# The forget gate's token products of a two-layer fused kernel: seven half-width blocks for each pair of sequences instead of plain products

## The chip, the cores and the metric

The kernel runs on one core of one Trainium2 chip. The metric is device time in microseconds (us) of one execution. The inputs are drawn once, with a fixed seed, and all arrays are float32.

## The reference, cut to what matters

The whole computation is two layers of a network on 32 sequences of 128 tokens with 512 channels. Most of it (a mixture of experts, a feed-forward part chosen per sequence, a second mixture of experts) comes before the part that the change touches and is left as it is. The last part is a recurrence that steps over the 32 sequences; each step treats all 128 tokens of one sequence as a batch:

```python
c0 = jnp.broadcast_to(in_c, (batch, in_c.shape[0]))
def step(c, xt):                       # xt: 128 tokens x 512
    ft = jax.nn.sigmoid(xt @ wf.T + c @ uf.T + bf)
    it = jax.nn.sigmoid(xt @ wi.T + c @ ui.T + bi)
    gt = jnp.tanh(xt @ wc.T + c @ uc.T + bc)
    c = ft * c + it * gt
    return (c, None)
c_final, _ = lax.scan(step, c0, x)
h = jnp.tanh(jnp.einsum('tbi,oi->tbo', x, wo) + c_final @ uo.T + bo)
```

The products `xt @ w.T` (called token products here) do not depend on the state `c`; the products `c @ u.T` do. So the token products can be made ahead of their step, or for two steps at once, and the others can't.

## The kernel before, in words

**Numbers.** Every float32 matrix operand is split into a rounded high part and a remainder (`split`: ACT copies the high part, L64; DVE subtracts, L65). A product is then three TensorE matmuls, high by high, high by low and low by high (`mm3`, L95), summed in PSUM. One matmul takes a stationary block of 128 x 128 (the tokens or the state) and a moving block of up to 512 weight columns. With 512 channels a full product is 4 blocks x 3 = 12 matmuls of 512 columns.

**Order.** The program is written as straight Python; a scheduler of the framework orders each engine's queue at compile time, by the order of the program and by when it reckons the operands and buffers ready. `tc.issue_after(x)` and `queue_behind(i, x)` put an instruction behind another on its engine's queue by hand; they are no waits on the chip beyond the order of the queue. `behind(both)` does this for the two instructions (ACT's and DVE's) of a split.

**The recurrence.** A step `t` has these parts:

- `from_c(t, n, ...)`: the state's product of gate n (c, i, f), 12 matmuls of 512 columns into a bank of PSUM (pool `ps_g`, 3 banks, tile `ps_c`, `ps_i`, `ps_f`).
- `gate(t, n, ...)`: DVE adds the bias or the token part out of PSUM (L1720), ACT applies the sigmoid or tanh (L1721), and for i DVE multiplies by the tanh gate (L1723).
- `new_c`: DVE multiplies f by the old state (L1726) and adds i times g (L1728). The last instruction is kept in `made`.
- `turn`: TensorE transposes the new state (4 transposes, tile `ptC`, L1647) and `split` makes the stationary operand `cT` of the next step.
- `gate_y(t + 3)` prepares the tokens of a later sequence: fetched rows times a gate (DVE, L1612), 4 transposes (tile `ptF`, L1620), a copy (L1626), a split into `zA`. `sums_z` makes, for every second sequence, the sums of token blocks that the seven-block form needs (DVE, L1637 to L1641), split into `zS`.

**Token products of c and i before.** Two steps 2n and 2n+1 and the gates c and i are taken together as a 2 x 2 product of blocks: rows are the two steps, the inner index is the two halves of 256 channels, columns are the gates c and i. That is done with seven block products (Winograd's form of Strassen's scheme) instead of eight. Each block product is 2 x 3 = 6 matmuls of 512 columns into a bank of the pool `ps_b` (3 banks, tiles `pA11`, `pA12`, `pS1` and so on, shown as `pA` and `pS`). `first_of_pair` makes five of them before the turn into an even step; its sums run on DVE at L1690 to L1695. `second_i` makes S3 T3 before the turn into an odd step, and its two sums (L1705, L1706) are put behind `made`; `second_c` makes A22 T4 after that turn (sum at L1711). The weights' combinations (T1 to T4) are formed once at the start, in `rest_of_weights`, during steps 0 and 1. Steps 0 and 1 use plain products.

**Token products of f before.** `plain(t + 1, ps, "f", True, False)` puts the 12 matmuls of f for the next step into the bank of `ps_f`, where `from_c` adds the state's product later. Only the bias is added by `gate`. It stands before the turn into an odd step and after the turn into an even step.

**The end.** After the last steps the tokens of all sequences are read back (`z_d`), four groups of 512 at a time, split (tile `zF`) and multiplied by `wo` (tile `poF`, function `unit`), and the last state by `uo` (tile `cu`). `wo` is fetched and split in step 28 into a buffer of the pool `zp`; the first group's tokens are fetched there too.

## Time and profile before

| what | value |
|---|---|
| time, 3 runs | median 2416.92 us, 2414.24 to 2421.07 |
| the profiled execution | 2416.54 us, its span 2414.9 us, so 1.6 us lie outside the span |
| granted TensorE clock, mean | 0.999 |
| TensorE matmul busy | 2393.2 us, 99% of the span |
| VectorE (DVE) busy | 1485.1 us, 61% |
| ScalarE (ACT) busy | 1079.8 us, 45% |
| recurrence in the trace | first state product at 1777.94 us, last at about 2315 us |

"Span" is the time from the first to the last instruction in the profile. TensorE (PE) has two rows: PE for the matmuls, PEld for loading the stationary block, which overlaps. A matmul's shown duration is its latency through a pipeline; what it costs a full engine is the distance from start to start. A group of lines in the timeline is a run of alike instructions on an engine, with its start, its length and the count after the x; a bracket at the end tells how long the engine was idle before it, and whom it waited for.

### The profile page before, as it was taken

Reading aid. Unit: us, or ns where it says so; the run is one execution under the profiler, and the core shown is the slowest. Engines: PE = TensorE matmul, PEld = TensorE weight load, DVE = VectorE, ACT = ScalarE, POOL = GpSimd, SP = SyncE. Lnnn points to the kernel's source line nnn. Section 1 sums busy time; section 2 is a strip of 40 time slices with the busy share of each in tenths; the row PEclk is TensorE's granted clock in tenths of the full one; section 3 lists DMA queues with packets and bytes.
Section 4 is the critical chain, followed back from the end, with each engine's and each line's share of the span. In section 5 each row is a group of like instructions: output and inputs, shape, how many; then the busy total and the mean of one; then the engine's idle time right before and its main releaser. Section 6 shows DMA issues by size and latency. Waiting matters only on the chain.

```text
span 2414.9 us, 36797 instructions
## 1 busy us (share of the span) xinstructions
PE 2393.2 (99%) x12792; PEld 2028.2 (84%) x12792; DVE 1485.1 (61%) x2548; ACT 1079.8 (45%) x1897; POOL 417.4 (17%) x461
## 2 busy tenths in 40 slices
PE   9999999999999999999999999999999999999999
PEld 6788888888887888888888889999988888888887
DVE  8797644456567445446455477776756666666664
ACT  5544633343223545445455466666643223223242
POOL 1000022222233233323222120000010000000012
PEclk9999999999999999999999999999999999999999
DMA  6445555457564334343243287677642111111165
GB/s 219 150 131 170 184 171 167 151 188 254 175 222 156 128 128 130 106 132 110 86 151 125 90 297 253 226 224 233 196 156 63 49 44 53 49 44 49 53 238 181
DMA packets 196383, 357.93 MB, mean 148 GB/s; under 512 B 37665, under 2 KB 70481, under 8 KB 193633
## 3 DMA queue, kind: packets, MB, share of 16 engines
q1 hardware_dynamic: 148224, 258.57, 32.0%
q0 software_dynamic: 36448, 75.95, 10.6%
q10 hardware_dynamic: 11520, 20.98, 2.4%
q8 instruction: 107, 1.75, 0.3%
q14 instruction: 84, 0.68, 0.1%
HBM read 377.08 MB, written 91.80 MB: 194 GB/s over the span
## 4 chain that ended last, share of the span: by engine, by line
PE 78%; DMA 1%; DVE 1%; issue 1%; ACT 1%; ACTq 0%; POOL 0%; DVEq 0%; POOLq 0%
PE phD L95 7%; PE poD L95 7%; PE po L95 7%; PE ps_f L95 7%; PE p L95 6%; PE pb L95 4%; PE ps_i L95 4%; PE ps_c L95 4%; PE poF L95 3%; PE pS L95 3%; PE pv L95 3%; PE acc L95 3%; PE pA L95 2%; PE pur L95 2%; PE por L95 2%
## 5 line engine op out<-in xcount | busy, mean ns | idle before, releaser
L65 DVE TENSOR_TENSOR wD<-rawD,wD 128x1024 fp32r<-128x1024 f32 x128 | 156.5, 1229 | 77.6 <-ACT wD L64 77.5
L95 PE MATMUL p<-xhl,swu 128*128 128x512 f32 x768 | 190.6, 400 | 5.7 <-ACT xhl L64 5.7
L95 PE MATMUL p<-xhl,kept_u 128*128 128x512 f32 x768 | 184.6, 394 | 1.2 <-DVE kept_u L65 0.7
L95 PEld LDWEIGHTS phD<-xe,wD 128*128 128x128 f32 x1536 | 183.2, 188 | 1.3
L95 PE MATMUL phD<-xe,wD 128*128 128x256 f32 x1536 | 183.5, 279 | 0.0
L95 PE MATMUL poD<-wD,hD 128*128 128x512 f32 x768 | 181.5, 392 | 0.0
L95 PEld LDWEIGHTS p<-xhl,swu 128*128 128x128 f32 x768 | 145.7, 192 | 36.8 <-ACT xhl L64 5.9
L95 PEld LDWEIGHTS p<-xhl,kept_u 128*128 128x128 f32 x768 | 141.9, 188 | 31.3 <-DVE kept_u L65 1.1
L95 PEld LDWEIGHTS poD<-wD,hD 128*128 128x128 f32 x768 | 141.9, 188 | 28.3
L64 ACT CAST wD<-rawD 128x1024 fp32r<-128x1024 f32 x128 | 133.6, 1047 | 52.7 <-PE poD L95 31.0
L305 POOL DMA_INDIRECT xg<-in_x_rows_dram,blk_t x71 | 68.1, 960 | 439.0 <-PE ptx L315 242.0
L1587 POOL DMA_INDIRECT y<-res_d,gat_i x32 | 35.8, 1118 | 472.9 <-DVE r L1612 394.3
L95 PE MATMUL pur<-r,xb 128*128 x792 | 110.6, 288 | 3.3 <-issue 1.5
L65 DVE TENSOR_TENSOR xb<-ptx,xb 128x512 fp32r<-128x512 f32 x68 | 47.0, 691 | 106.1 <-ACT xb L64 102.7
L95 PE MATMUL por<-r,hbr 128*128 x396 | 107.6, 407 | 0.5 <-ACT hbr L64 0.5
L95 PEld LDWEIGHTS pur<-r,xb 128*128 128x128 f32 x792 | 98.6, 188 | 5.6 <-issue 2.7
L95 PE MATMUL ps_c<-uc_hl,cT 128*128 128x512 f32 x384 | 96.3, 399 | 0.0
L95 PE MATMUL pb<-rT,Wo_hl 128*128 128x256 f32 x768 | 94.7, 281 | 0.3 <-DVE rT L65 0.2
L95 PE MATMUL ps_f<-wf_hl,z 128*128 128x512 f32 x384 | 94.5, 394 | 0.0
L95 PE MATMUL acc<-kept_d,as 128*128 128x512 f32 x384 | 93.6, 392 | 0.4 <-DVE as L65 0.2
L844 POOL DMA_INDIRECT o<-o_d,s_i x64 | 64.7, 1011 | 168.0 <-PE pth L864 82.9
L95 PE MATMUL pv<-w_recept_hl,xr 128*128 128x512 f32 x384 | 93.7, 392 | 0.0
(1048 smaller groups left out, 5130.5 us busy)
## 6 DMA issues: line engine op xcount, KB each, us to landing
rawD<-in_w_key_dram SPq DMA_DIRECT2D x64, 512.0 KB
rawD<-in_w_value_dram SPq DMA_DIRECT2D x64, 512.0 KB
swr<-in_sw_dram SPq DMA_DIRECT2D x120, 256.0 KB
o_d<-obr SPq DMA_DIRECT2D x66, 256.0 KB
rraw<-in_rw_dram SPq DMA_DIRECT2D x32, 256.0 KB
xc<-in_x_dram SPq DMA_DIRECT2D x32, 256.0 KB
hid_d<-o ACTq DMA_DIRECT2D x32, 256.0 KB
xh_d<-xc SPq DMA_DIRECT2D x32, 256.0 KB
```

The costliest lines, as they stand in the source:

```text
L64: first = nc.scalar.copy(hi, src).ins
L65: done = nc.vector.tensor_tensor(lo, src, hi.bitcast(F32), ALU.subtract).ins
L95: done = nc.tensor.matmul(ps, lhsT=left(hl, k), rhs=right(hr, k), start=start and k + n == 0, stop=stop and 3 * k + n == last,)
L305: nc.gpsimd.indirect_dma_start(out=xg[i], out_offset=None, in_=a["x_rows"], in_offset=bass.IndirectOffsetOnAxis(ap=blk_t[:, i : i + 1], ax ...
L844: nc.gpsimd.indirect_dma_start(out=o[n], out_offset=None, in_=o_d, in_offset=bass.IndirectOffsetOnAxis(ap=idx[:, b : b + 1], axis=0),)
L1587: got = nc.gpsimd.indirect_dma_start(out=y, out_offset=None, in_=res_d, in_offset=bass.IndirectOffsetOnAxis(ap=gat_i[:, b : b + 1], axis=0),)
```

## The change

The token products of f are made with seven blocks too, for two steps at once. Rows are again the two steps and the inner index the two halves of the channels; the columns are now the two halves of f's own 512 columns, so a block product is 6 matmuls of 256 columns. The two sequences of the first pair, and of the second, are made plainly (`plain_f`): with the weights kept as blocks, where the second half of the columns of the upper channels is held as the sum B11 + T1, that takes 30 matmuls of 256 columns for each sequence. The products no longer add up in the bank of `ps_f`; they go to banks of `ps_b`, and DVE adds them to a tile `fs[t]`, which `gate` then adds to `ps_f` in place of the bias.

Around that: `f_start` (A11 B11, A12 B21) and `f_second` (S3 T3) stand before the turn into an odd step, `f_third` (A22 T4) after it, `f_first` (S1 T1, S2 T2, S4 B22) after the turn into an even step; the sums of `f_start`, `f_second` and `plain_f` are queued behind the split of `cT`. f's weights are split in seven pieces of 512 elements per partition instead of two of 1024, three of them in `rest_of_weights`. `zA` loses the block A21 (kept for the first pair alone), `zS` has one buffer, which first holds f's raw weights, `sums_z` uses the tile `y` as its scratch, so `get_y` comes after it, and `hl` moves to another pool. At the end `wo`'s split moves from step 28 to step 30 and into the room that the token weights leave, two of the first group's four loads go with it, `uo`'s splits are put behind the first group's and behind the last state, and the last turn behind two of the first `unit`s.

```diff
+        BLOCKS = {(0, 0): 0, (0, 1): 1, (1, 1): 2}
+        def tokens(n, j, half):
+            return zA[n][:, BLOCKS[j, half]] if (j, half) in BLOCKS else a21[0]
...
+                zA[n] = zp.tile([P, 3, 2, K2, P], FR, tag="z", name=f"z_{n}")
...
-            s = gp.tile([P, 2, K2, P], F32, tag="sz", name=f"sz_{n}")
+            zS[n] = zp.tile([P, 4, 2, K2, P], FR, tag="zs", bufs=1, name=f"zs_{n}")
+            s = spare[2 * n + 1].rearrange("p (s k q) -> p s k q", s=2, k=K2)
...
+        def blocks_f(n, *todo):
+            ps = ps_b.tile([P, 2, HD], F32, tag="b", name=f"pf{todo[0][0]}_{n}")
+            for i, (which, w) in enumerate(todo):
+                left = left_of(which, n)
+                mm3(ps[:, i], lambda h, k: left[:, h, k, :], lambda h, k: wf[w][:, h, k, :], K2)
+            return ps
...
+        def f_start(n):
+            f1, p1 = f_tile(2 * n)
+            ps = blocks_f(n, ("A11", "B11"), ("A12", "B21"))
+            return [
+                nc.vector.tensor_tensor(p1, ps[:, 0], bias["f"][:, :HD], ALU.add).ins,
+                nc.vector.tensor_tensor(f1, ps[:, 1], p1, ALU.add).ins,
+            ]
+        def f_first(n, room):
+            u, v = room[:, :HD], room[:, HD:]
+            p1 = fs[2 * n][:, HD:]
+            ps = blocks_f(n, ("S1", "T1"), ("S2", "T2"))
+            last = blocks_f(n, ("S4", "B22"))
+            with tc.issue_after(made[0]):
+                nc.vector.tensor_tensor(v, ps[:, 0], bias["f"][:, HD:], ALU.add)
+                nc.vector.tensor_tensor(u, ps[:, 1], p1, ALU.add)
+                nc.vector.tensor_tensor(v, v, u, ALU.add)
+                nc.vector.tensor_tensor(p1, last[:, 0], v, ALU.add)
+            f_done[n] = u, v
...
-            v[n] = gp.tile([P, D], F32, tag="v" + n, name=f"v_{n}_{t}")
+            v[n] = fs.pop(t) if n == "f" else gp.tile([P, D], F32, tag="v" + n, name=f"v_{n}_{t}")
...
+            nc.vector.tensor_tensor(f22, f22, f12, ALU.subtract)
+            split_f("T2", f22)
+            nc.vector.tensor_tensor(f11, f22, f11, ALU.subtract)
+            nc.vector.tensor_tensor(f21, f21, f22, ALU.subtract)
+            split_f("T3", f11)
+            split_f("T4", f21)
...
-                plain(1, ps, "f", True, False)
+                plain_f(1)
             elif t < NB - 1:
                 if odd:
                     second_i(n)
-                    plain(t + 1, ps, "f", True, False)
+                    rest, adds = f_second(n) if n > 1 else (None, [])
+                    if n + 1 < NB // 2:
+                        adds += f_start(n + 1)
                 else:
                     first_of_pair(n)
+                    adds = [plain_f(t + 1)] if n == 1 else []
                 cT_next = turn(c, t + 1)
+                for i in adds:
+                    queue_behind(i, last_split[1])
                 if odd:
                     second_c(n)
+                    if rest:
+                        f_third(n, *rest)
+                elif n == 1:
+                    plain_f(t + 2)
...
                 else:
-                    plain(t + 1, ps, "f", True, False)
+                    f_first(n, rooms.pop(n))
...
+            if t == NB - 2:
+                sx.close()
+                sz.close()
+                op = sf.enter_context(tc.tile_pool(name="op", bufs=1, side="right", **kw))
...
+                for k, raw in enumerate(raws):
                     split(wo1[:, 0, k], wo1[:, 1, k], raw)
...
+        ahead = [unit(0, o) for o in range(KD)]
+        for i in turned_c:
+            queue_behind(i, ahead[1])
```

More of the change, by code (lines that the diff above doesn't have):

```diff
@@ L156, in tile_kernel @@
     used_i = const.tile([P, 1], I32, name="used_i")
-    hl = const.tile([P, KD, NB], F32, name="hl")
     bo3 = const.tile([P, KD], F32, name="bo3")
@@ L830, in tile_kernel @@
         new_i = po_p.tile([P, NB], I32, name="new_i")
+        hl = po_p.tile([P, KD, NB], F32, name="hl")
         ones = po_p.tile([P, P], F32, name="ones2")
@@ L1601, in tile_kernel @@
             first_got = get_y(b)
-        zp = sf.enter_context(tc.tile_pool(name="zp", bufs=2, **kw))
-        zA, zS, zts = {}, {}, {}
+        sz = sf.enter_context(ExitStack())
+        zp = sz.enter_context(tc.tile_pool(name="zp", bufs=2, **kw))
+        zA, zS, zts, a21 = {}, {}, {}, []
+        BLOCKS = {(0, 0): 0, (0, 1): 1, (1, 1): 2}
+        def tokens(n, j, half):
+            return zA[n][:, BLOCKS[j, half]] if (j, half) in BLOCKS else a21[0]
+        spare = {}
         def gate_y(b):
@@ L1613, in gate_y @@
             if j == 0:
-                z = zp.tile([P, 2 * KD * D], FR, tag="z", name=f"z_{n}")
-                zA[n] = z[:, : KD * D].rearrange("p (j h k q) -> p j h k q", j=2, h=2, k=KD)
-                zS[n] = z[:, KD * D :].rearrange("p (s h k q) -> p s h k q", s=4, h=2, k=K2)
+                zA[n] = zp.tile([P, 3, 2, K2, P], FR, tag="z", name=f"z_{n}")
                 zts[n] = first_p.tile([P, 2, KD, P], F32, tag="cT0", name=f"zt_{n}")
@@ L1623, in gate_y, with split_tokens @@
             zt = zts[n][:, j]
+            def split_tokens(t):
+                if j == 0:
+                    t = t.rearrange("p (a k) q -> p a k q", a=2)
+                    split(zA[n][:, 0:2, 0], zA[n][:, 0:2, 1], t)
+                    return
+                if n == 0:
+                    a21.append(gp.tile([P, 2, K2, P], FR, tag="a21", name="a21"))
+                    split(a21[0][:, 0], a21[0][:, 1], t[:, :K2])
+                split(zA[n][:, 2, 0], zA[n][:, 2, 1], t[:, K2:])
             if b < LEAD:
-                split(zA[n][:, j, 0], zA[n][:, j, 1], pt)
+                split_tokens(pt)
             nc.scalar.copy(zt, pt)
@@ L1629, in gate_y @@
             if b >= LEAD:
-                split(zA[n][:, j, 0], zA[n][:, j, 1], zt)
+                split_tokens(zt)
+            spare[b] = y
         def sums_z(n):
@@ L1645, in turn @@
             pt = ps_c.tile([P, KD, P], F32, tag="t", name=f"ptC_{t}")
-            for k in range(KD):
-                nc.tensor.transpose(pt[:, k, :], c[:, bass.ts(k, P)], ident)
+            turned_c[:] = [
+                nc.tensor.transpose(pt[:, k, :], c[:, bass.ts(k, P)], ident).ins for k in range(KD)
+            ]
             cT = gp.tile([P, 2, KD, P], FR, tag="cT", name=f"cT_{t}")
@@ L1653, in bank, with left_of @@
             return ps_g.tile([P, D], F32, tag="g", name=f"ps_{n}_{t}")
+        def left_of(which, n):
+            if which[0] == "S":
+                return zS[n][:, int(which[1]) - 1]
+            return tokens(n, int(which[1]) - 1, int(which[2]) - 1)
         def block(which, w, n):
-            s = {"A11": (0, 0), "A12": (0, 1), "A22": (1, 1)}.get(which)
-            if s is None:
-                left = zS[n][:, int(which[1]) - 1]
-            else:
-                left = zA[n][:, s[0], :, s[1] * K2 : (s[1] + 1) * K2]
+            left = left_of(which, n)
             ps = ps_b.tile([P, D], F32, tag="b", name=f"p{which}_{n}")
@@ L1664, in block, with f_tile @@
             return ps
+        HD = D // 2
+        def blocks_f(n, *todo):
+            ps = ps_b.tile([P, 2, HD], F32, tag="b", name=f"pf{todo[0][0]}_{n}")
+            for i, (which, w) in enumerate(todo):
+                left = left_of(which, n)
+                mm3(ps[:, i], lambda h, k: left[:, h, k, :], lambda h, k: wf[w][:, h, k, :], K2)
+            return ps
+        fs, f_done = {}, {}
+        def f_tile(t):
+            pool, tag = (gp, "vf") if t % 2 or t == 0 else (first_p, "c0")
+            fs[t] = pool.tile([P, D], F32, tag=tag, name=f"v_f_{t}")
+            return fs[t][:, :HD], fs[t][:, HD:]
@@ new lines, in plain_f @@
+        def plain_f(t):
+            n, j = divmod(t, 2)
+            f_tile(t)
+            ps = ps_b.tile([P, 2, HD], F32, tag="b", name=f"pf_{t}")
+            for i, todo in enumerate((((0, "B11"), (1, "B21")), ((0, "B11"), (0, "T1"), (1, "B22")))):
+                for m, (half, w) in enumerate(todo):
+                    z = tokens(n, j, half)
+                    mm3(
+                        ps[:, i], lambda h, k: z[:, h, k, :], lambda h, k: wf[w][:, h, k, :], K2,
+                        m == 0, m == len(todo) - 1,
+                    )
+            return nc.vector.tensor_tensor(fs[t], ps.rearrange("p i n -> p (i n)"), bias["f"], ALU.add).ins
@@ new lines, in f_start @@
+        def f_start(n):
[4 more added lines that the diff above has]
+                nc.vector.tensor_tensor(f1, ps[:, 1], p1, ALU.add).ins,
+            ]
+        def f_first(n, room):
[9 more added lines that the diff above has]
+            f_done[n] = u, v
@@ L1666, in plain, with f_second, f_third @@
+        def f_second(n):
+            f1, f2 = f_tile(2 * n + 1)
+            u, v = f_done.pop(n)
+            ps = blocks_f(n, ("S3", "T3"))
+            adds = [
+                nc.vector.tensor_tensor(u, ps[:, 0], u, ALU.add).ins,
+                nc.vector.tensor_tensor(f2, ps[:, 0], v, ALU.add).ins,
+            ]
+            return (f1, u), adds
+        def f_third(n, f1, u):
+            nc.vector.tensor_tensor(f1, blocks_f(n, ("A22", "T4"))[:, 0], u, ALU.add)
         def plain(t, ps, which, start, stop):
@@ L1671, in plain @@
                 "i": ((0, "B11"), (0, "T1"), (1, "B22")),
-                "f": ((0, "f0"), (1, "f1")),
             }[which]
@@ L1676, in plain @@
             for m, (half, w) in enumerate(todo):
-                z = zA[n][:, j, :, half * K2 : (half + 1) * K2]
+                z = tokens(n, j, half)
                 done = mm3(
@@ L1682, in plain @@
             return done
-        half_done, made = {}, []
+        half_done, made, rooms, turned_c = {}, [], {}, []
         def first_of_pair(n):
@@ L1689, in first_of_pair @@
             p1, u, v = first[:, 0], first[:, 1], second[:, 0]
+            rooms[n] = second[:, 1]
             nc.vector.tensor_tensor(p1, block("A11", "B11", n), bias["c"], ALU.add)
@@ L1729, in new_c @@
             return new
+        names = ("T4", "T3", "T2", "B22", "T1", "B21", "B11")
+        f_all = shifted(wx_p, len(names) * K2 * D, tag="wf", name="wf_hl")
+        f_all = f_all.rearrange("p (w h k n) -> p w h k n", w=len(names), h=2, k=K2)
+        wf = {n: f_all[:, i] for i, n in enumerate(names)}
         wt = {
             n: wx_p.tile([P, 2, K2 * D], FR, tag="w" + n, name=f"w{n}_hl")
-            for n in ("T4", "T3", "T2", "f1", "B22", "T1", "B21", "B11", "f0")
+            for n in names
         }
@@ L1761, in tile_kernel, with split_f @@
         for n in "cif":
-            from_c(0, n, ps, cT, True, False)
-        f01 = zp.tile([P, 2 * KD * D], F32, tag="z", name="raw_wf")
-        f01 = [f01[:, bass.ts(h, K2 * D)] for h in range(2)]
+            from_c(0, n, ps, cT, True, n == "f")
+        raw_f = zp.tile([P, KD, D], F32, tag="zs", bufs=1, name="raw_wf")
         with tc.issue_after(first_got):
             for h in range(2):
-                nc.gpsimd.dma_start(out=f01[h], in_=a["wf"].rearrange("p k n -> p (k n)")[:, bass.ts(h, K2 * D)])
+                s = slice(h * K2, (h + 1) * K2)
+                nc.gpsimd.dma_start(out=raw_f[:, s], in_=a["wf"][:, s])
+        f11, f12, f21, f22 = (raw_f[:, h * K2 : (h + 1) * K2, bass.ts(i, HD)] for h in range(2) for i in range(2))
+        def split_f(n, raw):
+            split(wf[n][:, 0], wf[n][:, 1], raw)
         gate_y(0)
@@ L1773, in tile_kernel @@
         with behind(first_z):
-            for h in range(2):
-                split_part(f"f{h}", f01[h])
+            split_f("B11", f11)
+            split_f("B21", f21)
+            nc.vector.tensor_tensor(f12, f12, f11, ALU.subtract)
+            split_f("T1", f12)
+            split_f("B22", f22)
         for b in range(LEAD):
@@ L1798, in tile_kernel @@
                 with tc.issue_after(done):
-                    plain(0, ps, "f", False, True)
+                    plain_f(0)
+                more["f"] = fs[0]
                 for n in "cif":
@@ L1802, in tile_kernel @@
             else:
+                more["f"] = fs[t]
                 for n in "cif":
@@ L1821, in tile_kernel @@
                     second_i(n)
-                    plain(t + 1, ps, "f", True, False)
+                    rest, adds = f_second(n) if n > 1 else (None, [])
+                    if n + 1 < NB // 2:
+                        adds += f_start(n + 1)
                 else:
                     first_of_pair(n)
+                    adds = [plain_f(t + 1)] if n == 1 else []
                 cT_next = turn(c, t + 1)
+                for i in adds:
+                    queue_behind(i, last_split[1])
                 if odd:
                     second_c(n)
+                    if rest:
+                        f_third(n, *rest)
+                elif n == 1:
+                    plain_f(t + 2)
+                    rooms.pop(n)
+                    b1, b2 = (bias["f"][:, bass.ts(i, HD)] for i in range(2))
+                    nc.vector.tensor_tensor(b2, b2, b1, ALU.subtract)
                 else:
-                    plain(t + 1, ps, "f", True, False)
+                    f_first(n, rooms.pop(n))
             else:
@@ L1833, in tile_kernel @@
                 gate_y(b)
+                if b % 2:
+                    sums_z(b // 2)
+                spare.pop(b)
                 if b + LEAD < NB:
                     get_y(b + LEAD)
-                if b % 2:
-                    sums_z(b // 2)
             if t == NB - 4:
-                wo1 = zp.tile([P, 2, KD, D], FR, tag="z", name="wo_hl")
+                raws = []
                 for k in range(KD):
-                    raw = yp.tile([P, D], F32, tag="yr"[k % 2], name=f"raw_wo{k}")
+                    raws.append(yp.tile([P, D], F32, tag="yr"[k % 2], name=f"raw_wo{k}"))
                     with tc.issue_after(last_r[0]):
-                        nc.sync.dma_start(out=raw, in_=a["wo"][:, k, :])
+                        nc.sync.dma_start(out=raws[k], in_=a["wo"][:, k, :])
+                first_z = first_p.tile([P, 2, KD, P], F32, tag="cT0", name="zr_0")
+                first_z = [first_z[:, j] for j in range(2)]
+                for j in range(2):
+                    nc.sync.dma_start(out=first_z[j], in_=z_d[0][j])
+            if t == NB - 2:
+                sx.close()
+                sz.close()
+                op = sf.enter_context(tc.tile_pool(name="op", bufs=1, side="right", **kw))
+                zp = sf.enter_context(tc.tile_pool(name="z0p", bufs=1, **kw))
+                uo1 = op.tile([P, 2, KD * D], FR, tag="uo", name="uo_hl")
+                wo1 = op.tile([P, 2, KD, D], FR, tag="wo", name="wo_hl")
+                for k, raw in enumerate(raws):
                     split(wo1[:, 0, k], wo1[:, 1, k], raw)
-                first_z = []
-                for j in range(GB):
+                for j in range(2, GB):
                     first_z.append(yp.tile([P, KD, P], F32, tag="yr"[j % 2], name=f"zr_0_{j}"))
                     nc.sync.dma_start(out=first_z[j], in_=z_d[0][j])
-        sx.close()
-        op = sf.enter_context(tc.tile_pool(name="op", bufs=1, side="right", **kw))
         pos, zr, x1s, zs = {}, {}, {}, {}
@@ L1888, in unit @@
             pos[g, o] = po = pool.tile([P, GT], F32, tag=tag, name=f"poF_{g}_{o}")
-            mm3(po, lambda h, k: wo1[:, h, k, bass.ts(o, P)], lambda h, k: zs[g][:, h, k, :], KD)
+            return mm3(po, lambda h, k: wo1[:, h, k, bass.ts(o, P)], lambda h, k: zs[g][:, h, k, :], KD)
         split_z(0)
-        uo1 = op.tile([P, 2, KD * D], FR, tag="uo", name="uo_hl")
-        for h in range(2):
-            s = bass.ts(h, K2 * D)
-            split(uo1[:, 0, s], uo1[:, 1, s], raw_part("uo", h))
+        first_z = tuple(last_split)
+        with behind(first_z), tc.issue_after(made[0]):
+            for h in range(2):
+                s = bass.ts(h, K2 * D)
+                split(uo1[:, 0, s], uo1[:, 1, s], raw_part("uo", h))
         uo1 = uo1.rearrange("p h (k n) -> p h k n", k=KD)
@@ L1901, in tile_kernel @@
         cT = cT_next
-        for o in range(KD):
-            unit(0, o)
+        ahead = [unit(0, o) for o in range(KD)]
+        for i in turned_c:
+            queue_behind(i, ahead[1])
         cu = gp.tile([P, KD, P], F32, tag="vc", name="cu")
@@ L1925, in tile_kernel @@
             if g + 1 < NG:
-                split_z(g + 1)
+                with behind(first_z) if g == 0 else nullcontext():
+                    split_z(g + 1)
             fetch_z(g + 3)
```

## The prediction

> **What bounds the kernel now.** I read the busy table of the page first, then busy time by windows over the recurrence, then TensorE's waits there, then the timeline of one pair of steps and of steps 0 and 1.

> ```profile
> PE 2393.2 (99%) x12792; PEld 2028.2 (84%) x12792; DVE 1485.1 (61%) x2548; ACT 1079.8 (45%) x1897; POOL 417.4 (17%) x461
> ```

> ```profile
> core 0: us, PE busy (x) PEld busy (x) DVE busy (x) ACT busy (x) POOL busy (x), PEclk, DMA share, GB/s
> ...
> 1800.00:1820.00 20.00, 19.83 (x94) 15.94 (x93) 16.74 (x24) 9.64 (x15) 2.10 (x2) 1.00 0.22 67
> 1820.00:1840.00 20.00, 19.96 (x92) 16.20 (x91) 14.06 (x23) 5.45 (x9) 2.10 (x2) 1.00 0.23 66
> ...
> 2000.00:2060.00 60.00, 60.00 (x279) 49.64 (x279) 39.66 (x63) 17.31 (x28) 3.69 (x4) 1.00 0.14 45
> ```

> TensorE is the bound: from 1840 to 2300 us it is never idle, at full clock, with DVE busy for 39.66 of 60 us. Only at both ends of the recurrence does it wait at all, 2.0 us in sum, as the waits show for 1700 us to the end:

> ```profile
> PE ptC L1647 <- DVE c L1728: 0.7, 1, 0.7
> PE ps_c L95 <- ACT z L64: 0.7, 1, 0.7
> ...
> ```

> So what TensorE is spared in the middle is worth its full price, and every new wait is paid in full. The change is a trade in matmul counts, for which I need the distance from start to start of matmuls of 512 and of 256 columns.

> ```profile
> 1500.89 11.47 PE L95 MATMUL phD<-xe,wD 128*128 128x256 f32 x96
> 1512.20 2.92 PE L95 MATMUL poD<-wD,hD 128*128 128x512 f32 x12
> ```

> 96 matmuls of 256 columns take 1512.20 - 1500.89 = 11.31 us, 0.1178 us each. In the recurrence 12 of 512 columns take 2.72 us (2037.34 to 2040.06 below), 0.2267 us each. Two halves thus cost 0.2356 us, 4% more than a whole.

> **Part 1, the 14 pairs from the third on.** Removed: 24 matmuls of 512 columns per pair, 24 x 0.2267 = 5.44 us. Added: 7 blocks x 6 = 42 of 256 columns, 42 x 0.1178 = 4.95 us. That is -0.49 us a pair, -6.9 us in all. The seven blocks save an eighth of the columns, and a third of that goes back to the halved width. The nearest rows for the price of 256 columns are phD (0.1178), pb (48 from 1154.18 to 1159.92, 0.1196, behind transposes) and pur (12 from 405.10 to 406.56, 0.122, behind transposes too); the 48 cu matmuls of 128 columns at 0.114 are a floor. I take phD, the longest clean stream with the same kind of operands; 0.122 over the 708 new matmuls would add 3.0 us, 0.114 would take off 2.7.

> [...]

> **Part 2, the four plain steps.** Each step's 12 matmuls of 512 columns (2.72 us) become 30 of 256 columns (3.53 us): +0.81 us, +3.3 us for four. All four lie where TensorE is nearly full.

> **Part 3, DVE.** New per pair are nine sums of 256 columns. The nearest rows are the sums of the tile sz, 0.42 us, and a 128 x 256 one out of PSUM (x<-pb) at 0.418; 9 x 0.42 = 3.8 us, less 0.27 us for the half split of the odd sequence's tokens (0.42 instead of 0.69). DVE goes from about 65% to about 76% of a pair's 33.2 us. That is hidden as long as the chain through the state is not held up. In the odd turn I check it:

> ```profile
> 2035.97 1.52 PE L95 MATMUL pS<-wT_hl,z 128*128 128x512 f32 x6
> 2037.34 2.89 PE L95 MATMUL ps_f<-wf_hl,z 128*128 128x512 f32 x12
> 2038.30 0.69 DVE L1728 TENSOR_TENSOR c<-v_f,v_i 128x512 f32<-128x512 f32 x1
> 2038.90 0.68 DVE L1705 TENSOR_TENSOR ta<-pS,ta 128x512 f32<-128x512 f32 x1
> 2039.51 0.68 DVE L1706 TENSOR_TENSOR pd<-pS,tb 128x512 f32<-128x512 f32 x1
> ...
> 2040.06 0.60 PE L1647 MATMUL ptC<-ident,c 128*128 128x128 f32 x4
> ...
> 2040.41 1.64 PE L95 MATMUL pA<-wT_hl,z 128*128 128x512 f32 x6
> ```

> After the last state product TensorE has S3 T3 and f's 12 matmuls to do, 4.09 us, until the transposes ptC at 2040.06. The new state is there at 2038.30 + 0.69 = 2038.99. The new cover is S3 T3 of c and i (1.37), f_second (6 x 0.118 = 0.71) and f_start (12 x 0.118 = 1.41): 3.49 us, so ptC could start at 2039.46, still 0.47 us behind the state. The sums of f stand behind the split of cT by hand, so they don't delay the state. The even turn has five blocks, 6.8 us, for the same chain; f_first (2.1 us) and ptF (0.35 us) cover cT's split, which takes 1.9 us from the start of ptC.

> What is late next is a bank. The three banks of ps_b are now all taken before the odd turn: S3 T3, f_second, f_start. A22, which follows ptC, needs the first of them, and that comes free when the sum pd ends, 2039.51 + 0.68 = 2040.19. TensorE would get there at 2039.46 + 0.35 = 2039.81. So the wait is 0.4 to 0.5 us if A22 stays where it is, and 0.1 us or nothing if ptF's transposes (0.35 us) are put ahead of it. f_third then needs the bank of f_second, free only after the split of cT and two sums, about 2042.2; if the next state product goes first, nothing is lost. I take 0.2 us a pair, nearer the lower end since the order can absorb most of it: +2.8 us, between 0 and 14 x 0.5 = 7.0.

> **Part 4, the start.** During steps 0 and 1 DVE is the scarce engine:

> ```profile
> 1820.44 1.52 PE L95 MATMUL pS<-wT_hl,z 128*128 128x512 f32 x6
> 1821.80 1.52 PE L95 MATMUL ps_f<-wf_hl,z 128*128 128x512 f32 x6
> 1822.63 0.69 DVE L1690 TENSOR_TENSOR ta<-pA,bc_bc 128x512 f32<-128x512 f32 x1
> 1823.23 0.68 DVE L1728 TENSOR_TENSOR c<-v_f,v_i 128x512 f32<-128x512 f32 x1
> 1823.37 1.23 PEld L95 LDWEIGHTS pS<-wT_hl,z 128*128 128x128 f32 x6 [0.47 <-DVE ta L1690]
> ```

> From 1807 to 1824 us DVE hardly pauses, and TensorE already waits 0.47 us for the sum ta to free a bank. rest_of_weights gains three differences and three splits, 6 x 0.62 = 3.7 us of DVE in pitch, ahead of the sums of zS in its queue; plain_f adds a sum (0.61) and the half split saves 0.27. zS, now in the raw weights' buffer, can only be written after the last of these. So ta, at 1822.63 now, moves to about 1827.3. TensorE's own work before it grows by the two plain steps (1.6 us) and by doing all of plain_f(2) there (3.5 us instead of 1.4): it would run out at 1825.4 with its three banks full (A11, A12, plain_f), and wait till 1828.0. That is 2.6 us instead of 0.5: +2.1 us, between 0 (if the queue lets ta go earlier) and 5 (if S2 and S4 wait too). At step 0 the four pieces of f's weights cost 0.4 us of ACT and 1.0 of DVE more, beside a pause of DVE for a fetch (3.7 us at 1796).

> **Part 5, the end.** wo's split (four of 0.69 us on DVE) and two of the first group's four loads now wait for the last block product of step 30, at about 2307; two loads of some 2 us follow the first splits, then their own splits. The first unit is due at 2315.26 in the present trace. I get 2314 to 2316 for its operand. Gained may be the 0.7 us for which ptC now waits at 2320.41, as two units stand ahead of it. +0.3 us, between -0.7 and +2. The later get_y in odd steps lies on POOL's queue some 14 us ahead of its use and costs nothing; without that cover it would cost up to the 3.35 us that DVE waited for the first such fetch, at 1785.92.

> **Sum** against the profiled 2416.54 us, which is 0.4 under the median: -6.9 + 3.3 + 2.8 + 2.1 + 0.3 = +1.6, so 2418.1 us. That is 0.07%; about 0.3% (7.2 us) is what a measurement here can tell from no change.

> **Rivals.** (a) The clean trade: no bank wait, DVE in order at the start, the pause at the end gone: -6.9 + 3.3 - 0.7 = -4.3, 2412.2 us. For it: TensorE has shown no wait in the middle at 65% DVE. Against: DVE is already late at the start. Only with the 256-column price near 0.114 as well does it pass 7.2 us. (b) The three banks become the bound in every pair: A22 waits 0.5 us, and f_third, kept in its place, waits 0.6 us more behind the split of cT: 14 x 1.1 = 15.4, and with the other terms -6.9 + 3.3 + 15.4 + 2.4 = +14.2, 2430.7 us, slower. It decides from (7.2 + 3.6 - 2.4) / 14 = 0.6 us of waits a pair. For it: the three banks and the late sums of f; against: ptF and the next state product can be put between. (c) The start costs 6 us instead of 2, since the backlog of DVE reaches the turn into step 3: 2422 us. That the products don't leave TensorE's path can be ruled out: it has no idle time to hide them in.

> **How the numbers follow.** Forecast 0.60, (a) 0.17, (b) 0.15, (c) 0.08. Faster by over 0.3% takes 0.05 out of (a); slower takes (b) and a little of (c), 0.16; the rest, 0.79, is within 0.3%. The range is 2411 to 2426: down to (a) with a slightly lower price of a matmul, up over (c) and the bounds of parts 3 to 5, leaving out most of (b).

> **What would show it.** Right: a pair's period of about 32.9 us instead of 33.2, matmuls of 256 columns 0.118 us apart, a wait of TensorE near 1825 to 1828 of 2 to 3 us for a bank, short waits of pA for a sum in odd turns. Wrong: waits of f's blocks or of pA over 0.6 us in each pair, 256 columns at 0.125 us or more, or first units that start past 2318.

## The result and the profile after

The kernel after takes 2427.07 us, median of 11 runs (2424.52 to 2429.65), the kernel before beside it 2416.92 (11 runs, 2412.52 to 2421.07). The ratio is 1.0040, with a 95% interval of 1.0033 to 1.0048: slower by 10.2 us. The forecast was 2418.1, no change, range 2411 to 2426. It was wrong. The profiled execution of after took 2428.18 us with a span of 2426.5, which is 11.6 more than the 2414.9 of before.

The busy row of the page, then busy time by windows (length, busy us and count of each engine, granted clock, DMA share, GB/s):

```profile
PE 2396.6 (99%) x13116; PEld 2042.2 (84%) x13116; DVE 1531.8 (63%) x2689; ACT 1077.3 (44%) x1903; POOL 412.1 (17%) x461
```

```profile
core 0: us, PE busy (x) PEld busy (x) DVE busy (x) ACT busy (x) POOL busy (x), PEclk, DMA share, GB/s
...
1820.00:1840.00 20.00, 17.31 (x92) 13.94 (x91) 15.22 (x28) 3.62 (x7) 2.09 (x2) 0.91 0.09 27
...
2000.00:2060.00 60.00, 60.00 (x321) 51.32 (x320) 43.52 (x78) 18.49 (x31) 3.81 (x4) 1.00 0.15 49
...
```

In the middle TensorE is as full as before, with 321 matmuls where there were 279, and DVE has gone from 39.66 to 43.52 of 60 us. What stands out is 1820 to 1840: 17.31 us busy instead of 19.96, and a granted clock of 0.91. TensorE's waits from 2290 us to the end, where the kernel before had only the 0.7 us of its last turn, show the second such place:

```profile
PE cu L95 <- ACT cu L2044: 1.9, 2, 1.4
PE poF L95 <- ACT zF L64: 0.5, 1, 0.5
PE ps_c L95 <- ACT cT L64: 0.3, 1, 0.3
PE poF L95 <- DVE zF L65: 0.2, 1, 0.2
```

I cut both spans at three marks: the first state product, the turn into step 4 (`ptC` at 1858.08 before, 1870.00 after), and the turn into step 30, 13 pairs later (2289.81 and 2297.25).

| stretch | before | after | difference | predicted for this cut |
|---|---|---|---|---|
| to the first state product | 1777.94 | 1780.57 | +2.6 | 0 |
| start, to the first mark | 80.14 | 89.43 | +9.3 | +6.8 |
| 13 pairs | 431.73 | 427.25 | -4.5 | -3.8 |
| end | 125.09 | 129.25 | +4.2 | -1.4 |
| sum | 2414.9 | 2426.5 | +11.6 | +1.6 |

The last column lays the prediction's terms over the same cut. The start gets the plain steps (+3.3), the wait (+2.1) and `f_start` of the first seven-block pair, which now lies ahead of the mark (12 x 0.1178 = +1.4). The end gets the last pair, whose 24 matmuls of 5.44 us became 30 of 3.53 us there (-1.9), its bank wait (+0.2) and the prediction's +0.3. So the pairs did slightly better than forecast, and the loss came from both ends (+2.5 and +5.6 over the forecast) and from ahead of the recurrence (+2.6).

**The start.** TensorE's timeline, then the two DVE rows that matter:

```profile
1821.49 3.11 PE L95 MATMUL pA<-wB_hl,z 128*128 128x512 f32 x12
...
1825.42 1.21 PE L95 MATMUL pS<-wT_hl,zs 128*128 128x512 f32 x4 [0.22 <-DVE zs L65]
1829.11 0.65 PE L1667 MATMUL ptC<-ident,c 128*128 128x128 f32 x4 [2.48 <-DVE c L1816]
1829.70 2.25 PE L95 MATMUL pS<-wT_hl,zs 128*128 128x512 f32 x6
1831.76 2.55 PE L95 MATMUL pS<-wB_hl,zs 128*128 128x512 f32 x6
1834.15 3.70 PE L95 MATMUL pf<-wf_hl,z 128*128 128x256 f32 x30
```

```profile
1828.37 0.68 DVE L1816 TENSOR_TENSOR c<-v_f,v_i 128x512 f32<-128x512 f32 x1
1828.97 0.68 DVE L1778 TENSOR_TENSOR ta<-pA,bc_bc 128x512 f32<-128x512 f32 x1
```

With its three banks full, TensorE has only the turn left, and the new state is ready at 1828.37 + 0.68 = 1829.05: a wait of 2.48 us. Then comes what no term of the sum held: the next 12 matmuls of 512 columns run from 1829.70 to 1834.15, 4.45 us instead of the 2.72 that 12 such take in the trace of before. Windows of 2 us show why:

```profile
1828.00:1830.00 2.00, 0.90 (x5) 0.71 (x6) 2.00 (x4) 0.20 (x1) 1.15 (x1) 1.00 0.00 0
1830.00:1832.00 2.00, 2.00 (x7) 1.58 (x6) 1.45 (x4) 0.38 (x1) 0.94 (x1) 0.63 0.47 131
1832.00:1834.00 2.00, 2.00 (x6) 1.51 (x6) 2.00 (x4) 0.00 (x0) 0.00 (x0) 0.52 0.43 131
1834.00:1836.00 2.00, 2.00 (x18) 1.96 (x17) 1.08 (x2) 0.00 (x0) 0.00 (x0) 1.00 0.00 0
```

The engine is busy for all of 2.00 us, but with 7 and 6 matmuls: the granted clock is at half for 3.4 us (the 0.63 and 0.52 of the two windows make 1.48 + 1.92 us), from 1830.5 to 1833.9.

**The end.** The chain there, from ACT's and TensorE's timelines:

```profile
2334.21 2.79 PE L95 MATMUL cu<-cT,uo_hl 128*128 128x128 f32 x24
2335.07 2.18 ACT L64 CAST zF<-zr 128x512 fp32r<-128x512 f32 x4 [5.05 <-DMA zr<-z_d]
...
2337.16 0.36 ACT L2044 ACTIVATE cu<-cu,bo_sb 128x128 f32<-128x128 f32 x1
...
2337.57 1.56 PE L95 MATMUL cu<-cT,uo_hl 128*128 128x128 f32 x12 [0.57 <-ACT cu L2044]
...
2340.50 2.82 PE L95 MATMUL cu<-cT,uo_hl 128*128 128x128 f32 x12 [1.37 <-ACT cu L2044]
```

The tokens come back in eight groups of 512 (four sequences each). The casts of the fourth group (`split_z`) stand ahead of cu's first activation in ACT's queue. They wait 5.05 us for their fetch. cu's third product needs a bank that this activation frees, so TensorE waits behind a transfer that it doesn't need. In the kernel before such casts stand ahead of it too, but the first four began at 2324.48, 34.7 us after the last mark, and cu's first product at 2327.51, 37.7 us after it, so the casts were out of the way. Here the casts begin 37.8 us after the mark and cu's first product 37.0. And the clock falls again, near 2339.1 (0.78 of the first window below), behind the first of the two waits; the second begins only at 2340.50 - 1.37 = 2339.13:

```profile
2338.00:2340.00 2.00, 1.13 (x11) 0.98 (x9) 1.64 (x4) 1.48 (x3) 0.00 (x0) 0.78 0.13 39
2340.00:2342.00 2.00, 1.50 (x7) 1.50 (x8) 2.00 (x4) 1.77 (x5) 0.00 (x0) 0.50 0.99 351
2342.00:2344.00 2.00, 2.00 (x9) 1.89 (x9) 1.47 (x3) 1.09 (x3) 1.58 (x1) 0.50 0.71 267
2344.00:2346.00 2.00, 2.00 (x6) 1.53 (x5) 1.29 (x2) 0.90 (x3) 0.01 (x1) 0.52 0.85 165
```

### The profile page after: what moved, and what is told of

It reads as the page before. It is cut to its first block, busy times and chain, and to the rows that moved or that the text cites. A ratio compares the mean times of both kernels' runs of the same rounds, so it can differ in the third digit from the quotient of the medians.

```text
span 2426.5 us, 37634 instructions
## 1 busy us (share of the span) xinstructions
PE 2396.6 (99%) x13116; PEld 2042.2 (84%) x13116; DVE 1531.8 (63%) x2689; ACT 1077.3 (44%) x1903; POOL 412.1 (17%) x461
## 4 chain that ended last, share of the span: by engine, by line
PE 77%; DVE 2%; DMA 2%; issue 1%; ACT 1%; ACTq 0%; POOL 0%; SPq 0%; DVEq 0%; POOLq 0%
PE po L95 7%; PE phD L95 7%; PE poD L95 7%; PE p L95 6%; PE pb L95 4%; PE ps_i L95 4%; PE ps_c L95 4%; PE poF L95 3%; PE pS L95 3%; PE pv L95 3%; PE ps_f L95 3%; PE acc L95 3%; PE pA L95 3%; PE pur L95 2%; PE por L95 2%; PE pfS L95 2%
## 5 line engine op out<-in xcount | busy, mean ns | idle before, releaser
L95 PE MATMUL p<-xhl,swu 128*128 128x512 f32 x768 | 188.7, 397 | 5.9 <-ACT xhl L64 5.9
L95 PE MATMUL p<-xhl,kept_u 128*128 128x512 f32 x768 | 184.5, 394 | 1.2 <-DVE kept_u L65 0.7
L95 PEld LDWEIGHTS phD<-xe,wD 128*128 128x128 f32 x1536 | 183.2, 188 | 1.3
L95 PE MATMUL poD<-wD,hD 128*128 128x512 f32 x768 | 182.1, 392 | 1.6 <-DVE hD L65 1.0
L95 PE MATMUL phD<-xe,wD 128*128 128x256 f32 x1536 | 183.5, 279 | 0.0
L95 PEld LDWEIGHTS p<-xhl,swu 128*128 128x128 f32 x768 | 144.3, 190 | 36.4 <-ACT xhl L64 6.1
L95 PEld LDWEIGHTS p<-xhl,kept_u 128*128 128x128 f32 x768 | 141.9, 188 | 31.3 <-DVE kept_u L65 1.1
L95 PEld LDWEIGHTS poD<-wD,hD 128*128 128x128 f32 x768 | 141.7, 188 | 30.6 <-DVE hD L65 1.4
L64 ACT CAST wD<-rawD 128x1024 fp32r<-128x1024 f32 x128 | 133.6, 1047 | 55.8 <-PE poD L95 49.3
L95 PE MATMUL pur<-r,xb 128*128 x792 | 110.4, 288 | 3.3 <-issue 1.6
L95 PE MATMUL por<-r,hbr 128*128 x396 | 107.7, 407 | 0.5 <-ACT hbr L64 0.5
L95 PEld LDWEIGHTS pur<-r,xb 128*128 128x128 f32 x792 | 98.4, 188 | 5.4 <-issue 2.5
L95 PE MATMUL ps_c<-uc_hl,cT 128*128 128x512 f32 x384 | 98.3, 398 | 0.3 <-ACT cT L64 0.3
L95 PE MATMUL acc<-swd,as 128*128 128x512 f32 x384 | 94.7, 391 | 1.2 <-ACT sh L625 0.7
L95 PE MATMUL pb<-rT,Wo_hl 128*128 128x256 f32 x768 | 94.7, 281 | 0.3 <-DVE rT L65 0.2
L95 PE MATMUL acc<-kept_d,as 128*128 128x512 f32 x384 | 93.2, 391 | 0.6 <-ACT as L64 0.4
L95 PE MATMUL pv<-w_recept_hl,xr 128*128 128x512 f32 x384 | 93.6, 392 | 0.0
L95 PE MATMUL ps_i<-ui_hl,cT 128*128 128x512 f32 x384 | 92.4, 389 | 0.0
```

Source lines behind the costliest of these rows:

```text
L64: first = nc.scalar.copy(hi, src).ins
L95: done = nc.tensor.matmul(ps, lhsT=left(hl, k), rhs=right(hr, k), start=start and k + n == 0, stop=stop and 3 * k + n == last,)
```

## The experiments

The theory from the profile after: the steady trade is as predicted, and the loss is two stalls at the ends, each made dearer by the clock that falls after it. The rivals: the moved tile `hl` shifts addresses or transfers ahead of the recurrence; slow matmuls at the start come from something other than the wait (DMA, operands just written); the trade itself loses. Runs e1 to e4 stood beside a before of 2416.23 (21 runs), e5 to e7 beside one of 2417.41 (27 runs).

**e1, the kernel before with `hl` moved alone.**

```diff
-    hl = const.tile([P, KD, NB], F32, name="hl")
...
+        hl = po_p.tile([P, KD, NB], F32, name="hl")
```

> The kernel before, with only the tile hl moved to the other pool, so that every tile behind it in the first pool lies 512 bytes lower. In the changed kernel's profile the recurrence began 2.6 us later (first state product at 1780.57 us instead of 1777.94), though up to there the order of instructions on each engine is the same. Theory A, the addresses cost it: this run starts the recurrence at about 1780.5 and is 2 to 3 us slower than the kernel before. Theory B, the transfers arrived later in that one execution: the start lies anywhere between 1777.5 and 1781, and the time is the same within 1 us.

Measured: 2416.10 us (11 runs, 2413.44 to 2418.84), ratio 0.9999 (0.9990 to 1.0008). The first state product started at 1776.9, earlier than in any other run. The move of `hl` costs nothing. Of the 2.6 us ahead of the recurrence 0.4 stand there by 1405 us (1405.11 and 1405.53), and the rest comes near 1431, at two waits of `poD` (0.65 and 0.95 us) behind late landings of the weight fetch `rawD` (ACT's casts of it waited 2.14 and 1.67 us between 1413 and 1421 us, 0.69 us at the same place in the kernel before). Such differences come and go with no edit there: the same stretch ended at 1777.94 and 1779.6 in two kernels with before's code up to that point, and at 1778.6 to 1781.7 in six with after's. Why the landings move isn't settled.

**e2, the kernel after with the gap filled.** Ten matmuls that nothing uses are put between the last block product and the waiting turn.

```diff
+            if n == 1:
+                fill = ps_g.tile([P, D], F32, tag="g", name="fill")
...
+                for j in range(10):
+                    filled = nc.tensor.matmul(fill, lhsT=uc["c"][:, 0, 0, :P], rhs=uc["c"][:, 0, 0, :], start=True, stop=True)
...
+                    queue_behind(turned_c[0], fills.pop())
```

> The changed kernel with ten extra matmuls of 512 columns (0.227 us each, results unused) put between the block S1 T1 of the second pair and the transposes of the turn into step 2, where TensorE waited 2.5 us for the state and the next twelve matmuls took 4.45 us instead of 2.72. Theory A, the wait costs twice, since the granted clock falls to one half for a while after it: the clock stays at 1.00 between 1826 and 1836 us, the twelve matmuls take 2.7 us, the turn does not move, and the kernel is 1.7 us faster than the changed one (2425.4). Theory B, the twelve matmuls are slow for another reason (operands, banks): they still take about 4.4 us and the time stays at 2427 or rises.

Measured: 2425.04 us (5 runs, 2424.18 to 2428.95), ratio 1.0038 (1.0024 to 1.0052). TensorE's timeline:

```profile
1827.67 2.44 PE L1785 MATMUL fill<-uc_hl 128*128 128x512 f32 x10
1830.32 0.66 PE L1667 MATMUL ptC<-ident,c 128*128 128x128 f32 x4 [0.21 <-DVE c L1825]
1830.92 1.67 PE L95 MATMUL pS<-wT_hl,zs 128*128 128x512 f32 x6
1832.43 1.55 PE L95 MATMUL pS<-wB_hl,zs 128*128 128x512 f32 x6
1833.82 3.70 PE L95 MATMUL pf<-wf_hl,z 128*128 128x256 f32 x30
```

The turn comes as late as before, 7.64 us after the start of pA (7.62 in after), but the 12 block products behind it take 2.90 us instead of 4.45 and the granted clock stays at 1.00. The same instructions with the same operands, and only 0.21 us of idle time ahead: the slow matmuls are due to the wait. In the time of the whole kernel the 1.6 us can't be seen, the interval is too wide; the verdict rests on the trace.

**e3, the kernel after with other banks at the start.** `plain_f` of steps 2 and 3 uses the state products' pool, so `ps_b` isn't full and TensorE has plain_f's work left while it waits for the state.

```diff
-            ps = ps_b.tile([P, 2, HD], F32, tag="b", name=f"pf_{t}")
+            pool, tag = (ps_g, "g") if t >= 2 else (ps_b, "b")
+            ps = pool.tile([P, 2, HD], F32, tag=tag, name=f"pf_{t}")
```

> The changed kernel with the plain products of f for steps 2 and 3 in the banks of the state products (pool ps_g) instead of ps_b. If the banks of ps_b are what leaves TensorE without work near 1826 to 1829 us (my prediction's part 4), the 30 matmuls of plain_f(2) fill the wait: wait 2.5 us gone, no fall of the clock, 4.2 us off the start, 2422.9 us. If the state's chain on DVE alone sets the pace there, the work only changes its place: the wait moves behind the turn and the time stays within 1 us of 2427.

Measured: 2422.26 us (11 runs, 2419.87 to 2424.89), ratio 1.0024 (1.0015 to 1.0033): 6.0 above its before, where after is 10.2 above its own. The timeline and a window:

```profile
1825.41 2.88 PE L95 MATMUL pf<-wf_hl,z 128*128 128x256 f32 x23
1828.13 0.60 PE L1667 MATMUL ptC<-ident,c 128*128 128x128 f32 x4
```

```profile
1826.00:1830.00 4.00, 4.00 (x32) 3.78 (x31) 4.00 (x8) 0.66 (x2) 1.85 (x2) 1.00 0.14 33
```

No wait, no fall of the clock, and the start takes 84.37 us instead of 89.43. The end is as long as in after (129.72), with waits of 0.64 and 1.56 us in cu.

**e4, the kernel before with waits of many lengths.** Between 3 and 7 further operations of DVE (the state's maximum with itself, which changes nothing) stand before 14 turns, and the block products, the A22 product and the gated tokens are held behind the turn, so that TensorE has nothing else to do.

```diff
+            if t % 2 == 0 and 2 <= t <= 28:
+                for _ in range((3, 4, 5, 6, 7)[(t // 2 - 1) % 5]):
+                    made[:] = [nc.vector.tensor_tensor(new, new, new, ALU.max).ins]
...
+                    with tc.issue_after(turned_c[0]):
```

> The kernel before with 3, 4, 5, 6 or 7 extra DVE operations on the new state (a maximum with itself, about 0.62 us each in a row) before the turn into each of 14 odd steps, and with TensorE's later work kept behind that turn, so that TensorE idles by steps of about 0.8, 1.4, 2.0, 2.6 and 3.3 us. Theory A, a long enough wait halves the granted clock for about 3.4 us: waits of 0.8 us leave the clock at 1.00, those of 2.6 and 3.3 us are followed by a stretch at about 0.5, and the time is 2416.9 + 28 us of waits + some 1.7 us for each clock fall (6 to 11 falls, 10 to 19 us), about 2455 to 2464. Theory B, no effect of waits on the clock: 1.00 everywhere in the recurrence, about 2445 us.

Measured: 2465.53 us, one run. Three waits of the timeline (the idle time stands in the bracket), and the window that follows each, in the same order:

```profile
2062.07 0.63 PE L1647 MATMUL ptC<-ident,c 128*128 128x128 f32 x4 [1.82 <-DVE c L1731]
...
1914.25 0.63 PE L1647 MATMUL ptC<-ident,c 128*128 128x128 f32 x4 [2.54 <-DVE c L1731]
...
2098.02 1.08 PE L1647 MATMUL ptC<-ident,c 128*128 128x128 f32 x4 [2.55 <-DVE c L1731]
```

```profile
2062.00:2064.00 2.00, 1.93 (x11) 1.64 (x12) 1.77 (x3) 0.59 (x1) 0.00 (x0) 1.00 0.00 0
...
1914.00:1916.00 2.00, 1.75 (x10) 1.55 (x11) 1.77 (x4) 0.59 (x1) 0.00 (x0) 1.00 0.00 0
...
2098.00:2100.00 2.00, 1.98 (x7) 1.81 (x8) 1.31 (x3) 0.59 (x1) 0.00 (x0) 0.50 0.00 0
```

After the six waits of 1.09 and 1.82 us the clock stayed at 1.00. Of three waits of 2.54 or 2.55 us one brought it down to 0.50. All five of 3.27 to 4.00 us did. Without a fall, the distance of two turns was 33.21 (the pair's own) plus the wait plus 0.19. After a fall it was longer by another 1.4 to 2.8 us: from 2098.02 to 2136.11, for example, 38.09 = 33.21 + 3.28 + 0.19 + 1.41.

The granted clock was 1.00 or 0.50 in this run, and the trace, which keeps the time of each change, has the six falls of the recurrence at 1950.92, 1988.47, 2097.69, 2135.24, 2176.20 and 2319.56. From one to the next that is 11, 32, 11, 12 and 42 times 3.413 us; the falls of after at 1830.52 and 2339.10 lie 149 times 3.413 us apart. Half clock lasted 3.41 us after four of the six and 6.83 us after two. Windows of e4 cut at these steps show what parted two of the waits of 2.54 and 2.55 us:

```profile
1909.96:1913.37 3.41, 1.75 (x8) 1.13 (x6) 3.27 (x5) 0.00 (x0) 0.00 (x0) 1.00 0.00 0
1913.37:1916.78 3.41, 2.53 (x15) 2.21 (x16) 3.05 (x6) 0.61 (x2) 0.00 (x0) 1.00 0.00 0
...
2094.28:2097.69 3.41, 1.19 (x6) 0.65 (x4) 3.27 (x5) 0.00 (x0) 0.00 (x0) 1.00 0.00 0
2097.69:2101.11 3.42, 3.09 (x10) 2.64 (x11) 2.07 (x4) 0.59 (x1) 0.00 (x0) 0.50 0.00 0
```

The edge at 1913.37 splits the first wait into 1.66 and 0.88 us of idle time, and the clock stays at 1.00. Of the second wait 2.22 us lie in one window, and the next window has 0.50. In the recurrence of this run the clock fell behind each such window at full clock with 2.22 us of idle time or more, and behind none with 1.82 us or less.

**e5, the kernel after with the activations of cu ahead of the casts of the fourth and fifth groups of tokens.**

```diff
-            nc.scalar.activation(cu[:, o, :], pc, AF.Identity, bias=bo1[:, o : o + 1])
+            cu_done = nc.scalar.activation(cu[:, o, :], pc, AF.Identity, bias=bo1[:, o : o + 1]).ins
...
-                with behind(first_z) if g == 0 else nullcontext():
+                with behind(first_z) if g == 0 else tc.issue_after(cu_done) if g in (2, 3) else nullcontext():
```

> The changed kernel, with ACT's splits of the end's third and fourth further groups of tokens (tile zF) queued behind the four activations of cu. In the changed kernel the first of these activations stood on ACT's queue behind four splits that waited 5.05 us for their fetch, TensorE waited 1.9 us for it, and the clock then lay at 0.5 from 2340 to 2346. Theory A, this order costs the end: both waits of cu go, the clock stays at 1.00, about 4 us off, 2423. Theory B, the wait for the fetch only moves to the next user of ACT: the waits move to poF and the time stays within 1 us of 2427.

Measured: 2422.19 us (11 runs, 2417.91 to 2425.53), ratio 1.0021 (1.0012 to 1.0030): 4.8 above its before. TensorE's timeline at the end:

```profile
2334.05 5.47 PE L95 MATMUL cu<-cT,uo_hl 128*128 128x128 f32 x48
2339.36 5.94 PE L95 MATMUL poF<-zF,wo_hl 128*128 128x512 f32 x25
```

All 48 products of cu run without a break, the clock is 1.00 in each window from 2336 to 2342, and the end takes 124.23 us instead of 129.25. The start kept its wait of 2.48 us and its fall of the clock.

**e6, the edits of e3 and e5 together.**

> The changed kernel with both mends: plain products of steps 2 and 3 in the banks of ps_g, and cu's activations ahead of the late splits. If start and end are the two causes and independent, the gains add up: 2427.1 - 4.8 - 4 = about 2418, with the clock at 1.00 from the start of the recurrence to the last matmul. If the kernel still lies over 2420, a third cause is left.

Measured: 2416.61 us (11 runs, 2414.25 to 2419.70), ratio 0.9997 (0.9988 to 1.0006). The start takes 84.46 us, 13 pairs 427.24, the end 124.16. So the gains add up within their intervals of about 2 us each (-4.1 and -5.4 apart, -11.0 together, each against its own before), and with both stalls gone the change is worth nothing that can be measured.

**e7, e6 with seven blocks for the second pair too.** The first of its blocks go to the state products' banks. This was to win back half of the plain steps' price.

```diff
...
-                    rest, adds = f_second(n) if n > 1 else (None, [])
+                    rest, adds = f_second(n)
...
-                    adds = [plain_f(t + 1)] if n == 1 else []
+                    adds = f_start(1) if n == 1 else []
...
```

> As e6, with seven blocks for the second pair as well instead of plain products (f_start of that pair in the banks of ps_g). TensorE has 2 x 0.81 + 0.49 = 2.1 us less work; but only 1.4 us of f's matmuls instead of 3.5 lie before the turn into step 2, so that up to 1.5 us of wait for the state may come back, too short for a fall of the clock. Work alone: 2 us faster than e6, about 2416. If the state's chain on DVE sets the pace there: the same as e6 within 1 us.

Measured: 2417.91 us (11 runs, 2416.59 to 2421.69), ratio 1.0004 (0.9995 to 1.0013). TensorE's timeline, then a window:

```profile
1824.96 0.75 PE L95 MATMUL pfA<-wf_hl,z 128*128 128x256 f32 x5
1827.39 0.66 PE L1667 MATMUL ptC<-ident,c 128*128 128x128 f32 x4 [1.68 <-DVE c L1818]
```

```profile
1826.00:1828.00 2.00, 0.61 (x4) 0.42 (x4) 2.00 (x5) 0.00 (x0) 1.00 (x1) 1.00 0.00 0
```

The 18 matmuls that are saved (2.1 us) come back as a wait of 1.68 us for the state, whose chain runs on a DVE that is busy for 2.00 of 2.00 us. At the start DVE is the bound, and the plain products of sequences 2 and 3 were cover for it. The clock stayed at 1.00 after this wait.

## Why the prediction was wrong

**Part 1, the 14 pairs: right.** The 30 matmuls of 256 columns of plain_f from 1798.02 to 1801.56 stand 0.118 us apart, as phD's did. A pair takes 262.92 / 8 = 32.87 us (eight pairs from 1870.00) instead of 33.21; 32.9 was forecast. Two side figures were off, and the miss does not rest on them: the floor of 0.114 us was taken from a shown length (5.47 / 48), while from start to start the 48 cu matmuls stand 5.31 / 48 = 0.111 us apart; and with 0.114 rival (a) comes to -4.3 - 2.7 = -7.0 us, just short of the 7.2 that it was said to pass.

**Part 2, the plain steps: right** in their number and price, 30 x 0.118 each. In e6, which has them without the stall, the start is 4.3 us longer than before: 3.3 for these steps, 1.4 for the moved `f_start`, less the 0.47 us that TensorE waited before.

**Part 3, DVE and the banks: right.** TensorE isn't idle in the middle, DVE has 43.52 of 60 us (73%, forecast 76%), and the bank shows as a wait of 0.20 us of the weight load, as taken; a pair gained 0.34 us where the matmuls alone would give 0.49. TensorE's timeline (and its weight load, PEld) in an odd turn:

```profile
2014.70 1.57 PE L95 MATMUL pfA<-wf_hl,z 128*128 128x256 f32 x12
...
2016.11 0.60 PE L1667 MATMUL ptC<-ident,c 128*128 128x128 f32 x4
...
2016.55 0.38 PE L1627 MATMUL ptF<-ident,r 128*128 128x128 f32 x2
2016.89 1.23 PEld L95 LDWEIGHTS pA<-wT_hl,z 128*128 128x128 f32 x6 [0.20 <-DVE pd L1794]
```

Two of ptF's transposes went ahead of A22, as the prediction thought possible. So rival (b), which held nearly all the chance of "slower", named a mechanism that did not come. Nor did (c)'s: TensorE has no wait at the turn into step 3.

**Part 4, the start: the wait was right, its price too small.** 2.6 us were forecast with the banks full, 2.48 came, a little earlier than thought once the later first product is taken off, and with the state as the last thing waited for instead of the sum ta. But this wait was not paid once: the granted clock fell to half behind it, and 12 matmuls took 1.7 us more. The term "+2.1, between 0 and 5" measured 9.3 - 3.3 - 1.4 = 4.6, of which 2.48 + 0.22 - 0.47 + 1.7 = 3.9 are these waits, less the one of before, and the slow matmuls. It lies inside its bounds, but the upper one was given for another reason (S2 and S4 waiting too), so that it held is luck.

**Part 5, the end: this step failed.** It followed the transfers of the first group of tokens to the first units and stopped there, and put the later groups at nothing; like part 4, it had no price for a fall of the clock. "+0.3, between -0.7 and +2" measured 4.2 + 1.9 - 0.2 = 5.9, three times its upper bound. The first units waited 0.55 and 0.19 us, and the pause at the last turn went, as forecast. The first unit started at 2322.20, past the 2318 that was named as a sign of being wrong, but that came from what lay ahead: it is 24.95 us after the turn into step 30, against 25.45 before. What was left out is the later groups: `split_z(1)` now stands behind the first group's splits and `uo`'s, its buffer comes free later, the fourth group's fetch goes out later (2329.79), and the casts that wait for it stand ahead of cu's activation. That gives 1.94 us of waits in cu. The half clock adds 1.3 us on cu's last 12 products (2340.50 to 2343.12, 2.62 us instead of a quarter of the 5.31 that 48 take in e5) and about 1.4 on poF until 2346 (half of the 2.8 us from 2343.12). e5 removes 5.0 us of the end with one edit of ACT's order, which shows the blocking; what it leaves of this term, 124.23 - 125.09 + 1.9 - 0.2 = 0.8, lies inside the bounds. That the fetch is late through its buffer is read from the traces and wasn't tried by itself: it goes out 0.02 us after the last subtraction of `split_z(1)` ends in the kernel before (2318.46 and 2318.48) and 0.03 us after it here (2329.76 and 2329.79).

**Ahead of the recurrence** nothing was forecast and 2.6 us came in the profiled execution; e1 shows that `hl`'s move is not their cause. In e6 this stretch was 0.7 us longer than before and the time equal.

The chances failed with part 5: "slower" had been given 0.16, nearly all of it to (b). A tail outside the steady pairs had no rival of its own.

## What to carry to other kernels

When a change alters the order or the buffers of a tail, follow every transfer to its last consumer, and look at what stands behind that consumer in its engine's queue: here casts that waited 5.05 and 1.01 us for a fetch held up cu's activations, and TensorE waited 0.57 and 1.37 us for these. Price a wait of TensorE of about 2.5 us or more not by its length alone but with a fall of the clock that may stand behind it, here another 1.4 to 2.8 us (it came behind three of five waits of 2.48 to 2.55 us, behind all five of 3.27 to 4.00 us, and behind no wait of 1.82 us or less in the recurrence); fill such a gap with real work (here by another bank) before filling it with anything else. And a trade that gains 1% in the steady loop must be summed with its price at the start and the end, which here took all of it (e6).

## What had not been expected of the hardware

The falls of after, e4 and e5 whose end the traces show lasted 3.41 or 6.83 us, one or two such windows. The same 12 products behind the same 2.48 us of waiting took 4.45 us in after, where half clock lasted 3.41 us, and 5.23 in e5 (1828.80 to 1834.03), where the wait reached 0.88 us into a second window and half clock lasted 6.83 us, from 1827.15 to 1833.97.

The idle time of a window does not part all cases. In e5 the clock fell at the start behind one with 1.82 us of it (0.22 and 1.60 us, up to 1827.15); behind three windows with 1.82 us in e4 it stayed at 1.00. At the end of after it fell behind a window with 0.57 us of idle time (2335.69 to 2339.10), which held matmuls of 128 columns; in e5 the 48 matmuls of cu without a wait kept 1.00. In e3 cu's last 12 products, behind waits of 0.64 and 1.56 us, took a shown 2.82 us, as the 12 at half clock in after did. What decides besides the idle time was not shown.
